# Queries and keys of two chunks by seven products instead of eight, units in pairs of chunks, and the rotation's last two operations on GpSimd

## The chip, the core and the metric

The kernel runs on one core of a Trainium2 chip. The core has five engines, each with its own queue of instructions, done in order: TensorE (PE, matrix products into PSUM; its weight loads are listed as PEld), VectorE (DVE), ScalarE (ACT), GpSimd (POOL) and SyncE (SP, which only issues transfers here). 16 DMA engines move data. SBUF and PSUM are the two memories on the core; PSUM has eight banks of 512 float32 values per partition, and GpSimd works on SBUF only. The metric is the time of one execution in microseconds (us).

## The reference

A transformer block of one attention layer and one small product, in float32, for four sequences (batches) of 1024 tokens with 512 features; 16 heads of 128. Cut to what matters:

```python
xn  = layernorm(x)
q   = apply_rope(rmsnorm(xn @ Wq  + bq,  qn_w), pos)       # 16 heads x 128
lk  = apply_rope(rmsnorm(xn @ Wlk + blk, kn_w), pos)       # local keys
lv  = xn @ Wlv + blv                                       # local values
entries = sum over each 4 tokens of softmax(xn @ Wcmp) * xn
ck, cv  = apply_rope(rmsnorm(entries @ Wk + bk, kn_w), ends), entries @ Wv + bv
sparse  = softmax over the 8 largest of q @ ck.T (causal)  @ cv
local   = softmax over the last 128 keys of q @ lk.T       @ lv
out = x + ((sparse + local) / 2) @ Wo + bo + fp8(xn / 2) @ fp8(input2 / 2) * 4
```

`apply_rope` turns the first 64 of 128 features of a head: with `x1` and `x2` the first and second 32 of them, `x1*cos - x2*sin` and `x1*sin + x2*cos`.

## The kernel before

A *chunk* is 128 tokens, so there are 32 (`NT`), eight per batch (`NCH`). A *unit* is one chunk and two heads, so there are 8 units per chunk (`NU`) and 256 in all (`NN`), numbered chunk by chunk: `place(n)` is `divmod(n, 8)`. The 512 x 512 weights of a unit's queries and keys (two heads of each) lie in `wqk_sb[u]`; they stay in SBUF, as do those of the values (`wlv_sb`) and of the output (`wo_sb`). Biases are folded into the first row of the weights after the first chunk (`fold_first_row`), and the tokens' first row is ones.

The kernel's order is written out by hand (`manual_schedule`): each engine does its instructions in the order in which the program issues them, and waits only on data. A loop over `s` holds the pipeline; step `s` works on several units at once. In the order of issue, step `s` has:

- `scores(s)`, PE (L754, L761, L764): queries times the previous chunk's keys, this chunk's keys, and the compressed keys.
- `keep_context(s-2)`, ACT (L939): copies the context out of PSUM.
- `weigh(s)`: DVE adds masks (L786), finds the eight largest (L807, L812), ACT takes exponentials (L814, L822).
- `queries(s+3)`, PE (L606): four products with the 512 columns of `wqk_sb[u]` into one of two banks `qp`.
- `normalize(s+2)`: DVE multiplies `qp` by `r` and the norm's weight into `th` (L634, four heads), and POOL begins the rotation (L337).
- `settle(s)`, DVE (L830 to L840), and `divide(s)`, ACT (L847, four operations): the probabilities.
- `rotate`'s rest for unit `s+2`, DVE (L339, then L341 and L342).
- `turn(s)`, DVE (L865, two transpositions of `probs` in 32x32 blocks) and a store to DRAM; `turn_keys(s+2)`, DVE (L687, L690) and four stores.
- parts of the preparation of a later chunk (`chunk_prep`: layer norm, transposition, compression), and of `chunk_eight` (the fp8 product), whose quantization is three DVE operations and four of POOL (L292 to L298), one at each call of `steps()`.
- `squares(s+3)` on ACT (L321) and `spread(s+3)` on POOL (L315, L316): sums of squares from `qp`, and from them `r`.
- `to_output(s-2)`, PE (L957); `values_of(s+1)`, PE (L712); `values(s-1)`, PE (L924).
- SP fetches the transposed probabilities (`fetch(s)`, L907) and keys (`fetch_keys(s+2)`, L705) back from DRAM.
- `keep_values(s+1)`, ACT (L724).

In the first eight units the transpositions are made by PE instead (`turn_here`, `turn_keys_here`). A float32 product is listed as two passes on PE. PSUM's eight banks: `qp` two, `sc` two, `pp` two (values and all small products), `out` one, `ctx` one. `scratch` is a tile of 128x512 with two buffers; the preparation's `xb` and the quantization's `qv` and `qm` share it. `ready` and `made` say at which step of which chunk the preparation and the compressed entries of a later one begin.

Of the kernel before, what the change touches and what calls it, by code (L numbers as in the profile page):

```python
# [38 lines left out]
def kernel(  # L39
# [34 lines left out]
    NN = NT * NU  # L74
    assert S // RATIO <= 2 * P and NU == 8 and HID == 512
# [10 lines left out]
    def scratch(name, shape=(P, 512), dtype=F32):  # L86
        return work.tile(list(shape), dtype, tag="scratch", name=name, bufs=2)

    def pp(name):
        return psum.tile([P, 512], F32, tag="pp", name=name, bufs=2)  # L90
# [5 lines left out]
    x_tiles, angles = {}, {}  # L96

    def load_x(t, purpose, extra=False):

        b, c = divmod(t, NCH)  # L100
        if extra:
            xt = scratch(f"x_{purpose}_{t}")
        else:
            xt = work.tile([P, HID], F32, tag="x", name=f"x_{purpose}_{t}")
        nc.sync.dma_start(xt, hidden[b, ts(c, P), :])
        x_tiles[purpose, t] = xt

    def load_angles(t):
        c = t % NCH
        cs = work.tile([P, ROPE], F32, tag="cs", name=f"cs_{t}")  # L110
        nc.sync.dma_start(cs, rope[ts(c, P), :])
        angles[t] = cs
# [10 lines left out]
    wqk_sb = [const.tile([P, KK, 512], F32, name=f"wqk_{u}") for u in range(NU)]  # L123
    wlv_sb = [const.tile([P, KK, 256], F32, name=f"wlv_{u}") for u in range(NU)]
    wo_sb = [const.tile([P, 2, HID], F32, name=f"wo_{u}") for u in range(NU)]

    def load_wqk(u, engine):
        for i, w in enumerate((Wq, Wlk)):
            engine.dma_start(
                wqk_sb[u][:, :, ts(i, 256)], w[:, ts(u, 256)].rearrange("(k p) n -> p k n", p=P)  # L130
            )
# [4 lines left out]
    def load_wo(u, engine):  # L136
        engine.dma_start(wo_sb[u], Wo[ts(u, 256), :].rearrange("(h p) n -> p h n", p=P))
# [13 lines left out]
    for k in range(KK):  # L151
        for i, w in enumerate((Wq, Wlk)):
            nc.sync.dma_start(wqk_sb[0][:, k, ts(i, 256)], w[ts(k, P), 0:256])
# [109 lines left out]
    def fold_first_row(u):  # L263
        w = wqk_sb[u]
        row = first_row.pop(u, None)
        if row is None:
# [3 lines left out]
                row, ident[:, 0:1].to_broadcast([P, P]), w[:, 0, :], start=True, stop=True  # L270
            )
        nc.vector.tensor_tensor(
            w, w, row.unsqueeze(1).to_broadcast([P, KK, 512]), ALU.subtract
        )
        for i, bias in enumerate((bq, blk)):
            nc.sync.dma_start(
                w[0:1, 0, ts(i, 256)], bias[ts(u, 256)].partition_broadcast(1)
            )

# [21 lines left out]
    w2_sb = const.tile([P, KK, HID], BF16, name="w2_sb")  # L301


    w2_raw = [wo_sb[NU // 2 + k][:, 0, :] for k in range(KK)]

    def round_w2():
        for k in range(KK):
            spare = wo_sb[NU // 2 + k][:, 1, :]
# [14 lines left out]
    def rotate(th, cs, nh, a, name, bb=None):  # L323
# [17 lines left out]
        nc.vector.tensor_tensor(x12[:, :, 0, :], a[:, :, 0, :], bb[:, :, 1, :], ALU.subtract)  # L341
        nc.vector.tensor_tensor(x12[:, :, 1, :], a[:, :, 1, :], bb[:, :, 0, :], ALU.add)  # L342


    GC = P // NE
    entries = {}
# [4 lines left out]
    def chunk_prep(t):  # L351
# [46 lines left out]
        log = work.tile([P, 1], F32, tag="log", name=f"log_{t}", bufs=1)  # L398
        row = work.tile([P, 2, BLK], F32, tag="row", name=f"row_{t}", bufs=1)
        red = work.tile([P, BLK // RATIO], F32, tag="red", name=f"red_{t}", bufs=1)  # L400
# [19 lines left out]
        if not t:  # L420
            add_tokens_here(row)
            return
# [21 lines left out]
        else:  # L444
            stores.append((pooled[g][i], few))
        yield "added"
# [31 lines left out]
    def turn_tokens_here(xt):  # L478
# [4 lines left out]
        xnT = work.tile([P, KK, P], F32, tag="xnT", name="xnT_0")  # L483
# [3 lines left out]
    def fetch_tokens(t):  # L487
        xnT = work.tile([P, KK, P], F32, tag="xnT", name=f"xnT_{t}")
# [5 lines left out]
        chunks[t] = xnT, xones[t % 2]  # L494


    xones = [const.tile([P, P], F32, name=f"xone_{i}") for i in range(2)]

    def fetch_with_ones(t):
        turned = tokens.pop(t).rearrange("i (b k) a j -> b i k (a j)", b=NB)  # L500
        for b in range(NB):
            lo = 0 if b else 1
            nc.sync.dma_start(
                xones[t % 2][b * BLK + lo : (b + 1) * BLK], turned[b, lo:, 0, :]
# [92 lines left out]
    def place(n):  # L597

        return divmod(n, NU)

    def queries(n):
        t, u = place(n)
        xnT, xone = chunks[t]
        qp = psum.tile([P, 512], F32, tag="qp", name=f"qp_{n}")
        for k in range(KK):
            nc.tensor.matmul(  # L606
                qp,
# [608 lines left out]
```

## Time and profile before

| what | value |
|---|---|
| median of 3 runs | 2641.59 us (2640.97 to 2642.03) |
| the profiled execution's span, first to last instruction | 2641.7 us |
| PE busy | 2609.3 us |
| DVE busy | 2213.4 us |
| ACT busy | 1390.9 us |
| POOL busy | 786.2 us |
| queries and keys on PE (L606, tokens and ones) | 709.8 + 258.3 us |
| the DMA engines' time taken by the main queue | 58.8% |
| mean granted TensorE clock | 0.999 |

Busy time is the time in which an engine has at least one instruction under way; instructions of one engine overlap a little at their ends. A group's line in the profile names source line, engine, operation, the tile written and those read, the shape and the number of instructions; behind the bar stand busy time, mean duration in ns and idle time before them. A line of the list of waits names the waiting instruction and the one waited for, then total us, number and longest. A line of the timeline names start, duration, engine, line, operation and, in brackets, idle time before it. The span of the profiled execution is as long as the runs' median.

### The profile page before, as it was taken

Reading aid. Unit: us, or ns where it says so; the run is one execution under the profiler, and the core shown is the slowest. Engines: PE = TensorE matmul, PEld = TensorE weight load, DVE = VectorE, ACT = ScalarE, POOL = GpSimd, SP = SyncE. Lnnn points to the kernel's source line nnn. Section 1 sums busy time; section 2 is a strip of 40 time slices with the busy share of each in tenths; the row PEclk is TensorE's granted clock in tenths of the full one; section 3 lists DMA queues with packets and bytes.
Section 4 is the critical chain, followed back from the end, with each engine's and each line's share of the span. In section 5 each row is a group of like instructions: output and inputs, shape, how many; then the busy total and the mean of one; then the engine's idle time right before and its main releaser. Section 6 shows DMA issues by size and latency. Waiting matters only on the chain.

```text
span 2641.7 us, 46868 instructions
## 1 busy us (share of the span) xinstructions
PE 2609.3 (99%) x11879; PEld 1784.3 (68%) x11879; DVE 2213.4 (84%) x8381; ACT 1390.9 (53%) x5560; POOL 786.2 (30%) x1128
## 2 busy tenths in 40 slices
PE   8999999999999999999999999999999999999998
PEld 4666666776666666767766666667666666676776
DVE  6888888889888888888888888888888888877886
ACT  3545545555555555555555555555555555555555
POOL 3522323223332223232233322233323322322222
PEclk9999999999999999999999999999999999999999
DMA  8356556666655555666655555666665555566554
GB/s 255 110 156 162 151 145 175 171 176 158 164 143 154 162 155 156 169 173 170 166 157 144 158 149 158 177 164 164 171 176 147 150 148 153 147 168 171 159 152 110
DMA packets 722252, 422.20 MB, mean 160 GB/s; under 512 B 395823, under 2 KB 671552, under 8 KB 721984
## 3 DMA queue, kind: packets, MB, share of 16 engines
q1 hardware_dynamic: 721952, 419.20, 58.8%
q8 instruction: 97, 1.59, 0.3%
q14 instruction: 171, 1.40, 0.2%
q10 hardware_dynamic: 32, 0.02, 0.0%
HBM read 225.80 MB, written 193.20 MB: 159 GB/s over the span
## 4 chain that ended last, share of the span: by engine, by line
PE 84%; DVE 7%; ACT 3%; DMA 3%; SPq 2%; issue 1%; POOL 0%; ACTq 0%; DVEq 0%
PE qp L606 28%; PE op L957 14%; PE vp L712 14%; PE cp L924 13%; PE sc L764 5%; PE sc L761 4%; PE sc L754 4%; ACT prob L847 1%; ACT prob L814 1%; PE fp L588 1%; DVE sc L786 1%; DVE probB L865 1%; PE ep L536 1%; SPq L695 1%; DVE taken L812 1%
## 5 line engine op out<-in xcount | busy, mean ns | idle before, releaser
L606 PE MATMUL qp<-wqk,xnT 128*128 128x512 f32 x1552 | 709.8, 593 | 3.0 <-DMA wqk<-in_L_attn_Wlk_dram 2.4
L814 ACT ACTIVATE prob<-sc,neg 128x256 f32<-128x256 f32 (+1 forms) x512 | 235.9, 461 | 773.3 <-DVE taken L812 744.0
L606 PEld LDWEIGHTS qp<-wqk,xnT 128*128 128x128 f32 x1552 | 295.0, 190 | 372.5 <-issue 368.8
L847 ACT ACTIVATE prob<-prob,tot 128x256 f32<-128x256 f32 (+7 forms) x1024 | 382.0, 443 | 294.5 <-DVE tot L840 294.5
L712 PEld LDWEIGHTS vp<-wlv,xnT 128*128 128x128 f32 x2048 | 389.0, 190 | 161.3 <-issue 116.2
L957 PE MATMUL op<-wo,cT 128*128 128x512 f32 x1024 | 481.6, 593 | 4.2 <-ACT cT L939 4.2
L712 PE MATMUL vp<-wlv,xnT 128*128 128x256 f32 x2048 | 483.6, 379 | 0.0
L337 POOL TENSOR_TENSOR rb<-th,cs 128x256 f32<-128x256 f32 x256 | 203.8, 796 | 740.0 <-DVE th L634 733.2
L786 DVE CUSTOM_DVE_ANT_0 sc<-sc,mask_b 128x256 f32<-128x256 f32 (+1 forms) x512 | 211.6, 414 | 172.7 <-PE sc L764 162.7
L957 PEld LDWEIGHTS op<-wo,cT 128*128 128x128 f32 x1024 | 193.6, 190 | 229.8 <-issue 186.8
L865 DVE STREAM_TRANSPOSE probB<-prob 128x512 f32<-128x512 f32 (+2 forms) x490 | 305.8, 629 | 11.5
L315 POOL TENSOR_SCALAR r<-ss 128x4 f32<-128x4 f32 x256 | 61.9, 242 | 843.3 <-ACT junk L321 840.6
L924 PE MATMUL cp<-probT,lv 128*128 128x128 f32 x1920 | 299.0, 276 | 6.4 <-DMA probT<-pr 4.9
L321 ACT ACTIVATE junk<-qp 128x128 bf16<-128x128 f32 x1024 | 278.6, 272 | 28.9 <-PE qp L614 4.5
L924 PEld LDWEIGHTS cp<-probT,lv 128*128 128x128 f32 x1920 | 272.8, 191 | 25.4 <-issue 9.3
L634 DVE SCALAR_TENSOR_TENSOR th<-qp,r,norm_w 128x128 f32<-128x128 f32 x1024 | 286.1, 342 | 0.7 <-POOL r L316 0.4
L316 POOL TENSOR_TENSOR r<-r,nhalf 128x4 f32<-128x4 f32 x256 | 265.6, 1037 | 21.4
L830 DVE SCALAR_TENSOR_TENSOR prob<-taken,prob 128x128 f32<-128x128 bf16 (+7 forms) x512 | 186.4, 365 | 98.1 <-ACT prob L822 96.6
L606 PE MATMUL qp<-wqk,xone 128*128 128x512 f32 x496 | 258.3, 602 | 0.9 <-DMA xone<-xb_dram 0.7
L924 PE MATMUL cp<-probT,cv 128*128 128x128 f32 x1536 | 255.1, 275 | 0.0
L764 PE MATMUL sc<-ckT,qT 128*128 128x96 f32 (+7 forms) x1024 | 226.4, 303 | 0.0
L924 PEld LDWEIGHTS cp<-probT,cv 128*128 128x128 f32 x1536 | 212.7, 192 | 0.0
(141 smaller groups left out, 3674.9 us busy)
## 6 DMA issues: line engine op xcount, KB each, us to landing
pr<-probB SPq DMA_DIRECT2D x125, 512.0 KB
probT<-pr SPq DMA_DIRECT2D x500, 128.0 KB
qk<-thb SPq DMA_DIRECT2D x992, 64.0 KB
pr<-probB SPq DMA_DIRECT2D x96, 384.0 KB
probT<-pr SPq DMA_DIRECT2D x384, 96.0 KB
qT<-qk SPq DMA_DIRECT2D x248, 128.0 KB
lkT<-qk SPq DMA_DIRECT2D x248, 128.0 KB
x_norm<-_attn_hidden_states_dram SPq DMA_DIRECT2D x32, 256.0 KB
```

What stands on the lines that cost most here:

```text
L316: nc.gpsimd.tensor_tensor(r, r, nhalf[: ss.shape[0], 0:n], ALU.pow)
L321: nc.scalar.activation(junk[: src.shape[0]], src, AF.Square, accum_out=acc)
L606: nc.tensor.matmul(qp, xnT[:, k, :] if k or not t else xone, wqk_sb[u][:, k, :], start=(k == 0), stop=(t > 0 and k == KK - 1),)
L634: nc.vector.scalar_tensor_tensor(th[:, i, :], qp[:, ts(i, D)], r[:, i : i + 1], norm_w[:, i // 2, :], ALU.mult, ALU.mult,)
L712: nc.tensor.matmul(vp[:, 0:256], xnT[:, k, :], wlv_sb[u][:, k, :], start=(k == 0), stop=(k == KK - 1),)
L764: nc.tensor.matmul(sc[:, spa], q, ckT[:, 0:m], start=True, stop=True)
L786: nc.vector.tensor_tensor_reduce(sc[h][:, loc], sc[h][:, loc], mask_b[:, loc], -1.0, TAKEN, ALU.add, ALU.min, neg[h][0],)
L814: nc.scalar.activation(probs[h][:, loc], sc[h][:, loc], AF.Exp, bias=neg[h][0], scale=-1.0, accum_out=tot[:, h, 0:1],)
L847: nc.scalar.mul(probs[h][:, cols], probs[h][:, cols], tot[:, h, part : part + 1])
L865: nc.vector.transpose(pb[:, :, ds(h * g, g), :], prob[:, parts[0] * P : (parts[-1] + 1) * P].rearrange("p (g b i) -> p b g i", b=NB, i=BLK),)
L924: nc.tensor.matmul(blocks(cp[:, h, :]), v, probT[:, :, h * len(parts) + i - parts[0], :], start=(i == parts[0]), stop=(i == parts[-1]),)
L957: nc.tensor.matmul(op, cT[:, h, :], wo_sb[u][:, h, :], start=(u == 0 and h == 0), stop=(u == NU - 1 and h == 1),)
```

## The change

*Seven products.* For two chunks (256 tokens) and one unit's weights (512 x 512: 256 columns of queries, 256 of keys), the product is a 2x2 scheme of blocks: tokens of chunk a and chunk b, features in two halves, columns in queries and keys. Winograd's form of Strassen's algorithm takes seven block products and fifteen sums. Four sums of weight blocks per unit are made once (`combine_weights`, on POOL in steps 4 to 8), kept in DRAM (`combined`), and loaded for each unit pair into `places`. Four sums of tokens per pair of chunks are made on POOL (`sum_tokens`). The seven sums of results are four on POOL, after four copies by ACT (`first_sums`), and three on DVE straight from PSUM (`second_sums`). The first two chunks are computed as before.

*Order of units.* From the 17th unit on, units of two chunks alternate: chunk 2p unit u, chunk 2p+1 unit u. In an even step `first_products` (four products of 256 columns, two halves each) takes the place of `queries`, in an odd step `second_products` (three); they fill four quarters of two banks, `qk_banks`. `squares` and `normalize` read `th` in SBUF then, and `normalize` writes it in place.

*Rotation.* The last two operations of `rotate` (L341, L342) go to GpSimd for the units; the compressed keys' stay on DVE.

*Buffers.* `out` has two banks, `pp` one, and values and context share one (`vc`). `wo` is not kept whole but loaded per unit, then per unit pair, into two tiles. `scratch` has four buffers, `th` three tiles, tokens four. Preparation, entries and loads get new steps (`prep_at`, `made`, `tokens_at` and others), one chunk's preparation spread over six steps.

The diff, cut to its core:

```diff
+    def row_of_weights(u, k):
+        return wqk_sb[u][:, k // 2, :, k % 2, :]
...
+    def combine_weights(u):
+        (b11, b12), (b21, b22) = (
+            [flat(wqk_sb[u][:, j, i]) for i in range(2)] for j in range(2)
+        )
+        one, two = (v.rearrange("p h d -> p (h d)") for v in th_tiles[1:])
+        sub = nc.gpsimd.tensor_tensor
+        sub(one, b12, b11, ALU.subtract)
+        nc.sync.dma_start(combined[u][0], one)
+        sub(two, b22, one, ALU.subtract)
+        nc.sync.dma_start(combined[u][1], two)
+        sub(one, b21, two, ALU.subtract)
+        nc.sync.dma_start(combined[u][3], one)
+        sub(two, b22, b12, ALU.subtract)
+        nc.sync.dma_start(combined[u][2], two)
+    places = [flat(wqk_sb[u][:, 0, 1]) for u in range(NU)]
...
+    def load_combined(u, which):
+        for i in which:
+            nc.sync.dma_start(places[i], combined[u][i])
+    def sum_tokens(p, which):
...
+        op = nc.gpsimd.tensor_tensor
+        if which == 0:
+            op(s3, a11, a21, ALU.subtract)
+            op(s1, a21, a22, ALU.add)
+            op(s2, s1, a11, ALU.subtract)
+        else:
+            op(s4, a12, s2, ALU.subtract)
...
-        nc.vector.tensor_tensor(x12[:, :, 0, :], a[:, :, 0, :], bb[:, :, 1, :], ALU.subtract)
-        nc.vector.tensor_tensor(x12[:, :, 1, :], a[:, :, 1, :], bb[:, :, 0, :], ALU.add)
+        adder = nc.gpsimd if nh > 1 else nc.vector
+        adder.tensor_tensor(x12[:, :, 0, :], a[:, :, 0, :], bb[:, :, 1, :], ALU.subtract)
+        adder.tensor_tensor(x12[:, :, 1, :], a[:, :, 1, :], bb[:, :, 0, :], ALU.add)
...
-        return divmod(n, NU)
+        if n < FIRST:
+            return divmod(n, NU)
+        p, r = divmod(n, FIRST)
+        return 2 * p + r % 2, r // 2
...
+    def first_products(p, u):
+        xa, one = chunks[2 * p]
+        s1, s2, s3, _ = token_sums
+        t1, t2, t3, _ = (v.rearrange("p (k n) -> p k n", k=2) for v in places[:4])
+        lo, hi = qk_banks
+        product(lo[:, 0:256], (one, xa[:, 1, :]), wqk_sb[u][:, 0, 0])
+        product(hi[:, 256:512], both(s1), t1)
+        product(lo[:, 256:512], both(s2), t2)
+        product(hi[:, 0:256], both(s3), t3)
+    def second_products(p, u):
+        xa, xb = chunks[2 * p][0], chunks[2 * p + 1][0]
+        lo, hi = qk_banks
+        product(lo[:, 0:256], both(xa[:, 2:4, :]), wqk_sb[u][:, 1, 0])
+        product(hi[:, 0:256], both(xb[:, 2:4, :]), places[3].rearrange("p (k n) -> p k n", k=2))
+        product(hi[:, 256:512], both(token_sums[3]), wqk_sb[u][:, 1, 1])
...
+    def first_sums(n):
+        for i in (n, n + 1):
+            units[i] = {"th": pools["th"].take(i)}
+        c11, c12, c21, c22 = quarters(n)
+        lo, hi = qk_banks
+        nc.scalar.copy(c11, lo[:, 0:256])
+        nc.scalar.copy(c22, lo[:, 256:512])
+        nc.scalar.copy(c21, hi[:, 0:256])
+        nc.scalar.copy(c12, hi[:, 256:512])
+        nc.gpsimd.tensor_tensor(sums, c11, c22, ALU.add)
+        nc.gpsimd.tensor_tensor(c21, c21, sums, ALU.add)
+        nc.gpsimd.tensor_tensor(c22, c21, c12, ALU.add)
+        nc.gpsimd.tensor_tensor(c12, c12, sums, ALU.add)
+    def second_sums(n):
+        c11, c12, c21, _ = quarters(n)
+        lo, hi = qk_banks
+        nc.vector.tensor_tensor(c11, c11, lo[:, 0:256], ALU.add)
+        nc.vector.tensor_tensor(c21, c21, hi[:, 0:256], ALU.add)
+        nc.vector.tensor_tensor(c12, c12, hi[:, 256:512], ALU.add)
...
+    prep_at = {1: -1, 2: 6, 3: 8, 4: 13, 5: 16, 6: 19, 7: 22}
...
+        if s + 3 < FIRST:
+            for_unit(s + 3, (queries,))
+        if strassen and s != FIRST - 4:
+            (second_products if odd else first_products)(*pair_of)
...
         if s + 2 >= NU:
             for_unit(s + 2, (turn_keys,))
+        if strassen:
+            (second_sums if odd else first_sums)(2 * pair)
         steps()
-        host = t if u < 4 else t + 1
...
+        prepare(s, 0)
         for_unit(s + 3, (squares, (0, 1, 2, 3)), (spread,))
         for_unit(s - 2, (to_output,))
         steps()
+        prepare(s, 1)
...
+        if 0 <= s <= FIRST:
+            load_wo(s, nc.sync)
+        elif s > FIRST and odd:
+            load_wo(s + 1, nc.sync)
...
+        for v in {4: (0, 1), 5: (2, 3), 6: (4, 5), 7: (6,), 8: (7,)}.get(s, ()):
+            combine_weights(v)
+        if s == FIRST - 5:
+            load_combined(0, range(4))
+            spare_banks[:] = [pp_bank]
+        if strassen:
+            if odd:
+                load_combined((pair_of[1] + 1) % NU, (3,))
+            else:
+                load_combined((pair_of[1] + 1) % NU, (0, 1, 2))
```

## The prediction

> **What bounds the kernel now.** I read the page first: how long each engine is busy. Then the list of waits: who waits for whom. Then the timeline of single steps, to see how far the second-busiest engine is from the first.
>
> ```profile
> span 2641.7 us, 46868 instructions
> PE 2609.3 (99%) x11879; PEld 1784.3 (68%) x11879; DVE 2213.4 (84%) x8381; ACT 1390.9 (53%) x5560; POOL 786.2 (30%) x1128
> ```
>
> PE sets the pace. DVE is not 16% behind it, though, because part of DVE's idle time is spent on answers from ACT. What DVE waits for PE is this:
>
> ```profile
> DVE sc L786 <- PE sc L764: 162.7, 166, 2.1
> ...
> DVE qm_x L288 <- DMA pooled<-xb: 8.8, 3, 3.3
> DVE xb L378 <- DMA pooled<-xb: 7.8, 3, 2.6
> ...
> PE cp L924 <- DMA probT<-pr: 4.9, 9, 0.9
> ```
>
> So a PE of no length would leave 2641.7 - 162.7 = 2479.0 us: DVE's own line, 6% under the span. The reader should also see two short waits for a buffer (`scratch`), and that transfers arrive just in time (4.9 us in nine waits).
>
> PE's prices, from one step of the third chunk (columns: start, duration, engine, line):
>
> ```profile
> 1503.90 1.05 PE L606 MATMUL qp<-wqk,xone 128*128 128x512 f32 x2
> ...
> 1504.79 2.74 PE L606 MATMUL qp<-wqk,xnT 128*128 128x512 f32 x6
> ...
> 1507.36 1.03 PE L588 MATMUL fp<-w_sb,x 128*128 128x512 bf16 x4
> ...
> 1509.94 1.89 PE L712 MATMUL vp<-wlv,xnT 128*128 128x256 f32 x8
> ...
> 1511.67 0.61 PE L924 MATMUL cp<-probT,lv 128*128 128x128 f32 x4
> ```
>
> Starts count, since ends overlap. Four products of 512 columns are 8 passes and take 1507.36 - 1503.90 = 3.46 us, 0.4325 each; eight passes of 256 columns take 1511.67 - 1509.94 = 1.73 us, 0.216 each: exactly half, and longer than the 0.19 us of a weight load.
>
> DVE's step, between the reciprocal and the next step (fourth chunk):
>
> ```profile
> 1626.41 0.18 DVE L840 RECIPROCAL tot<-tot 128x4 f32<-128x4 f32 x1
> 1626.59 0.42 DVE L339 TENSOR_TENSOR thb<-th,cs 128x256 f32<-128x256 f32 x1
> 1626.68 1.49 ACT L847 ACTIVATE prob<-prob,tot 128x256 f32<-128x256 f32 x4 [0.87 <-DVE tot L840]
> ...
> 1627.12 0.29 DVE L341 TENSOR_TENSOR th<-thb,rb 128x128 f32<-128x128 f32 x1
> 1627.32 0.28 DVE L342 TENSOR_TENSOR th<-thb,rb 128x128 f32<-128x128 f32 x1
> 1627.53 1.26 DVE L865 STREAM_TRANSPOSE probB<-prob 128x384 f32<-128x384 f32 x2
> ...
> 1628.71 0.40 DVE L687 STREAM_TRANSPOSE thb<-th 128x256 f32<-128x256 f32 x1
> ...
> 1629.03 0.40 DVE L690 STREAM_TRANSPOSE thb<-th 128x256 f32<-128x256 f32 x1
> ...
> 1631.09 0.43 DVE L786 CUSTOM_DVE_ANT_0 sc<-sc,mask_b 128x256 f32<-128x256 f32 x1 [1.65 <-PE sc L764]
> ```
>
> The reader should see that ACT's four divisions end at 1628.17, and that the second half of L865 (about 0.6 of its 1.26 us) needs the last of them. The two rotation operations at 1627.12 and 1627.32 run while ACT divides.
>
> **The change, part by part.** One profiled execution lasts 2641.7 us; the runs' median is 2641.59, so nothing has to be added. 120 of the 128 unit pairs use the new products.
>
> *PE.* A pair took 16 x 0.4325 = 6.92 us and will take 28 x 0.216 = 6.05 (7 products, 2 halves, 2 passes): -0.87, times 120 = -104. PE's line becomes 2537.
>
> *DVE, three sums a pair.* The nearest row is `kv<-ep,bkv_sb` (L547), 128x256 from PSUM and SBUF, 0.386 us alone. In a row, L634 (0.343) comes every 0.26, so 0.31 apart: 0.31 + 0.31 + 0.386, less the overlap with what goes before, 0.95. +114 (bounds 84, for 0.7, and 139, for three times 0.386).
>
> *Rotation's end on GpSimd.* It takes 0.41 us from DVE per unit (1627.12 to 1627.53), 98 us over 240 units if all of it were on the path. By the rows above ACT covers it, and the transposition still waits until 1628.17: I take 0, bounds 0 and -98. On POOL the two cost some 0.46 each (L337: 0.322 for 64 elements, 0.732 for 256), done before L687 starts, so no new wait there. Normalizing from SBUF instead of PSUM is shorter at most; the second L830 waits 0.41 for ACT anyway.
>
> *ACT.* Four copies a pair at L724's 0.366: +176 on 1390.9, inside its idle time. But on ACT's queue the squares stand behind them, and in odd steps behind DVE's sums.
>
> *POOL.* Four sums of 0.73 and four rotation operations a pair: 4.8 x 120 = +570; busy share about 55%. What counts is what it holds up:
>
> ```profile
> 1567.16 1.28 POOL L294 TENSOR_TENSOR qv_x<-qv_x,qm_x 128x512 f32<-128x512 f32 x1
> ...
> 1567.36 1.11 DVE L839 TENSOR_SCALAR tot<-tot 128x4 f32<-128x4 f32 x1
> ```
>
> L839 takes 0.17 us and is held until POOL's operation ends. All L839s take 92.6 us instead of 256 x 0.170 = 43.5. After the change the quantization's POOL operations stand behind the rotation, which comes after L839: -45 (bounds 0 and -49). In exchange they stand in front of `r`. Third chunk, even step, from the start of L786: reciprocal ends at 5.0, divisions at 6.6, two copies at 7.4, POOL's four sums at 10.3, `r` (0.2 + 1.03) at 11.6; the next normalization is due at about 9.2 + 2.5 = 11.7. With L294 (1.27) and L296 (0.62) in between it is 1.8 late, of which ACT's 0.41 covers part: 1.4 per chunk. The sum of `x` and the bias adds some 0.6, chunk preparation on DVE and POOL's sums holding each other another 1.0. 3.0 x 30 chunks = +90. Bounds: 0, since L634 today is 0.343 beside any POOL operation, and +180, twice as much. I take the middle because `normalize` will read only SBUF, as L839 does.
>
> [...]
>
> *Start.* Combining weights is 32 POOL operations of 1.27 us; two of four also wait some 0.7 for a store of the buffer that they overwrite: 6.45 a unit, 52 in steps 4 to 8. In that stretch (77.0 to 140.9) POOL is busy 27.7 of 63.9 us; 36 are free, the rotation needs 5, and the units' `r` and rotation queue behind. At least 52 - 31 = 21; I take +25 (0 to 40). The four `scratch` buffers end the waits for `pooled`: -17 (0 to -17), hidden by nothing, since DVE waits hardly for PE there.
>
> *Transfers.* 1.5 MB a pair (four combined weights, one `wo`): 189 MB. The fullest slice moves 255 GB/s, so 740 us of the queue's time at that pace, on top of 58.8% of the span: over 80%. They are issued on SP behind `fetch_keys`, when SP waits for the next L865. 0 taken; bounds 0 and +60.
>
> *PSUM waits.* `first_products` waits for the first of the three sums only. PE's odd step is short (6.0 us plus scores and values, 8.8 in the third chunk), and DVE reaches that sum at 7.8 + 0.4 = 8.2 in the third chunk: no wait in itself.
>
> Sum on DVE's line: 2479.0 + 114 + 0 - 45 + 90 + 25 - 17 = 2646, plus a twentieth of today's waits for PE (8): **2654 us**.
>
> **Rivals.**
> - *The gain stays* (the other side). DVE's step gets shorter by the rotation: place L865, price 98 us. It decides if L865 after the change starts and ends earlier by over 0.2 us after the reciprocal. Then DVE's line is near 2556 and PE's is 2537 + 25 - 17 = 2545; with some of the lateness left, 2580. For: 0.41 us fewer instructions. Against: 1628.17.
> - *Transfers become late.* The store of `probB` queues behind combined weights; today a fetch is issued by 1507.4 and used about 1511.7. If half of 240 steps slip by 0.5 us: +60, 2714. For: the share over 80%. Against: only 4.9 us of such waits today.
> - *Half as wide is not half as long*, so the change saves PE nothing: 2700. Against: L712.
>
> **How the numbers follow.** DVE's line decides: 0.46 (own range 2635 to 2680); the gain stays: 0.34; transfers: 0.15; the last: 0.05. The range, 2585 to 2715, takes in half the rotation's bound below (-49 and the chunk term 20 smaller) and the transfer term above. About 0.2%, 5.3 us, is what a measurement can tell: faster 0.34 + 0.06 of the first case's lower end = 0.40; within 0.2% 0.09; slower 0.51.
>
> **What would show it.** Right: PE's busy share falls to some 96%, L606 is replaced by 256-column groups of 0.216 us spacing; DVE's share rises past 86% and its waits for PE's scores nearly vanish; L839's mean drops towards 0.17; L865 still ends 2.2 us after the reciprocal; PE waits for DVE's sums or POOL's results; steps 4 to 8 are longer. Wrong: PE still at 99% with a span below 2590 (then DVE had more room than I count), or new PE waits for `probT` or `qT`.

## The result and the profile after

The changed kernel takes 3030.1 us (median of 4 runs, 3028.9 to 3037.2), the kernel before, measured beside it, 2641.3 us: a ratio of 1.148 (95% interval 1.146 to 1.150). Slower was forecast, at 2654 us with a range up to 2715. The size is off by 376 us. The direction held, but slower had been given a chance of 0.51 and faster one of 0.40, so that says little.

The head of the page of the changed kernel:

```profile
span 3028.7 us, 52949 instructions
...
PE 2717.5 (90%) x13266; PEld 2124.7 (70%) x13301; DVE 2261.3 (75%) x8229; ACT 1567.8 (52%) x6032; POOL 1421.8 (47%) x2198
```

PE's share fell further than the 96% forecast, and not because DVE took over: DVE's share fell too, from 84% to 75%. PE is even busy 108 us longer than before, in part at a lower clock (below), although its queries and keys now need 28 passes of 256 columns a pair instead of 16 of 512. No engine is busy throughout; all of them wait. The list of waits (waiting instruction, the one waited for, total us, number, longest):

```profile
DVE thb L868 <- POOL th L434: 146.3, 20, 9.6
...
DVE sc L970 <- PE sc L946: 125.7, 81, 13.4
...
PE qk L743 <- DVE th L791: 123.3, 67, 6.1
...
DVE probB L1049 <- ACT prob L1031: 116.6, 231, 0.7
ACT th L779 <- DVE thb L868: 115.6, 108, 1.2
DVE th L814 <- POOL r L407: 108.9, 92, 5.6
...
DVE x L464 <- POOL off L459: 64.6, 16, 4.8
...
PE qk L743 <- DMA wqk<-combined: 35.4, 22, 3.9
...
PE vc L1115 <- DMA probT<-pr: 22.0, 25, 2.1
```

Before, DVE waited for PE's scores (162.7 us), for ACT's exponentials (96.6 us) and for little else. Now DVE waits for POOL in three places (L868, L814, L464: 319.8 us), PE for DVE (123.3 us), DVE for PE: a ring. A quiet step of a batch's third chunk, with the beginning of the next step, still looks much as forecast (start, duration, engine, line):

```profile
1108.84 2.75 PE L743 MATMUL qk<-wqk,wqk 128*128 128x256 f32 x12
...
1113.82 0.18 DVE L1024 RECIPROCAL tot<-tot 128x4 f32<-128x4 f32 x1
1114.00 0.43 DVE L430 TENSOR_TENSOR thb<-th,cs 128x256 f32<-128x256 f32 x1
1114.09 1.44 ACT L1031 ACTIVATE prob<-prob,tot 128x256 f32<-128x256 f32 x4 [0.91 <-DVE tot L1024]
1114.57 0.45 POOL L433 TENSOR_TENSOR th<-thb,rb 128x128 f32<-128x128 f32 x1 [1.11 <-DVE thb L430]
...
1114.90 1.25 DVE L1049 STREAM_TRANSPOSE probB<-prob 128x384 f32<-128x384 f32 x2 [0.48 <-ACT prob L1031]
...
1116.07 0.40 DVE L868 STREAM_TRANSPOSE thb<-th 128x256 f32<-128x256 f32 x1
...
1121.90 1.14 DVE L814 SCALAR_TENSOR_TENSOR th<-th,r,norm_w 128x128 f32<-128x128 f32 x4 [1.13 <-POOL r L407]
```

Twelve products of 256 columns take 2.75 us, 0.216 apart. The reciprocal ends at 1114.00, ACT's divisions end at 1115.53, the transposition L1049 cannot end before that: the rotation, taken from DVE, had been in ACT's shadow. And in the last line `r` is 1.1 us late. Elsewhere the same ring breaks wide open. Step 11 of each 16, same view:

```profile
1151.05 0.72 POOL L356 TENSOR_TENSOR wqk<-tokens,tokens 128x256 f32<-128x256 f32 x1 [8.79 <-DMA tokens<-xb_dram]
...
1154.91 0.45 DVE L868 STREAM_TRANSPOSE thb<-th 128x256 f32<-128x256 f32 x1 [6.96 <-POOL th L434]
...
1156.04 1.78 PE L743 MATMUL qk<-wqk,tokens 128*128 128x256 f32 x4 [4.01 <-DVE th L791]
...
1157.61 3.84 PE L743 MATMUL qk<-wqk,wqk 128*128 128x256 f32 x12
```

POOL waits 8.8 us for a transfer of tokens, DVE's transposition 7 us for POOL, PE 4 us for DVE. The twelve products after that take 3.84 us instead of 2.75: the clock has dropped. The granted clock is 1.00 from 1146.2 to 1156.0 us, 0.50 from 1156.4 to 1159.7, and 1.00 again from 1160 on. The view of the cores gives its mean:

```profile
core 0: 3028.7 us, clock 0.968
```

It was 0.999 before. A loss of 3.2% of 3029 us is 97 us of full clock, or 194 us at half. PE is busy in only 149 of these 194 us, so the lower clock makes PE's own work longer by some 75 us at most, and how much of that lies on the path no run shows. The Trainium skill (TensorE: Matmul & The Clock Gate, Part 1, "What's actually happening") says that the clock is halved after an idle window of some 3.4 us. The 3.84 us behind a gap of 4.0 us agree; no run here measures the window.

The steps' lengths, counted between first starts of the mask operation (L786, now L970), locate the loss: the first 16 steps take 245.5 us instead of 176.2 (+69); the later groups of 16 some 171 to 195 instead of 148 to 172, some 22 more each, 14 times.

### The profile page after: what moved, and what is told of

It is laid out like the page before. It is cut to its first block, busy times and chain, and to the rows that moved or that the text cites. A ratio compares the mean times of both kernels' runs of the same rounds, so it can differ in the third digit from the quotient of the medians.

```text
span 3028.7 us, 52949 instructions
## 1 busy us (share of the span) xinstructions
PE 2717.5 (90%) x13266; PEld 2124.7 (70%) x13301; DVE 2261.3 (75%) x8229; ACT 1567.8 (52%) x6032; POOL 1421.8 (47%) x2198
## 3 DMA queue, kind: packets, MB, share of 16 engines
q1 hardware_dynamic: 828176, 621.15, 71.9%
## 4 chain that ended last, share of the span: by engine, by line
DVE 28%; PE 28%; ACT 15%; POOL 10%; issue 8%; DMA 8%; SPq 4%; ACTq 0%; POOLq 0%; DVEq 0%
PE qk L743 8%; ACT prob L1031 7%; PE vc L1115 5%; PE out L1146 4%; PE vc L894 4%; DVE prob L1014 3%; DVE sc L970 3%; ACT prob L998 3%; DVE th L814 3%; DMA pr<-probB 2%; DVE taken L996 2%; DVE thb L868 2%; DVE top L991 2%; POOL r L407 2%; DMA wqk<-combined 2%
## 5 line engine op out<-in xcount | busy, mean ns | idle before, releaser
L743 PE MATMUL qk<-wqk,tokens 128*128 128x256 f32 x1440 | 385.3, 402 | 184.5 <-DVE th L791 123.3
L1146 PE MATMUL out<-wo,cT 128*128 128x512 f32 x1024 | 501.3, 613 | 53.9 <-ACT cT L1131 50.6
L894 PEld LDWEIGHTS vc<-wlv,tokens 128*128 128x128 f32 x2048 | 393.3, 192 | 171.7 <-issue 125.7
L894 PE MATMUL vc<-wlv,tokens 128*128 128x256 f32 x2048 | 488.5, 382 | 4.7 <-ACT lv L906 4.7
L743 PE MATMUL qk<-wqk,wqk 128*128 128x256 f32 x1860 | 466.1, 397 | 3.9 <-DMA wqk<-combined 3.9
L412 ACT ACTIVATE junk<-th 128x128 bf16<-128x128 f32 x960 | 299.4, 312 | 298.0 <-DVE th L791 275.0
L743 PEld LDWEIGHTS qk<-wqk,tokens 128*128 128x128 f32 x1440 | 262.5, 195 | 246.7 <-DVE th L791 141.1
L743 PEld LDWEIGHTS qk<-wqk,wqk 128*128 128x128 f32 x1860 | 374.7, 202 | 62.6 <-issue 4.6
L1049 DVE STREAM_TRANSPOSE probB<-prob 128x512 f32<-128x512 f32 (+2 forms) x490 | 310.0, 633 | 135.7 <-ACT prob L1031 116.6
L814 DVE SCALAR_TENSOR_TENSOR th<-th,r,norm_w 128x128 f32<-128x128 f32 x960 | 307.3, 381 | 103.3 <-POOL r L407 103.1
L1115 PE MATMUL vc<-probT,lv 128*128 128x128 f32 x1920 | 314.3, 283 | 23.8 <-DMA probT<-pr 22.0
L970 DVE CUSTOM_DVE_ANT_0 sc<-sc,mask_b 128x256 f32<-128x256 f32 (+1 forms) x510 | 209.6, 411 | 134.6 <-PE sc L946 125.7
L1115 PE MATMUL vc<-probT,cv 128*128 128x128 f32 (+3 forms) x1536 | 292.6, 291 | 0.0
```

What stands on the lines that cost most here:

```text
L412: nc.scalar.activation(junk[: src.shape[0]], src, AF.Square, accum_out=acc)
L743: nc.tensor.matmul(to, a[k], b[:, k, :], start=k == 0, stop=k == 1)
L814: nc.vector.scalar_tensor_tensor(th[:, i, :], qp[:, i, :], r[:, i : i + 1], norm_w[:, i // 2, :], ALU.mult, ALU.mult,)
L894: nc.tensor.matmul(vp, xnT[:, k, :], wlv_sb[u][:, k, :], start=(k == 0), stop=(k == KK - 1),)
L970: nc.vector.tensor_tensor_reduce(sc[h][:, loc], sc[h][:, loc], mask_b[:, loc], -1.0, TAKEN, ALU.add, ALU.min, neg[h][0],)
L1049: nc.vector.transpose(pb[:, :, ds(h * g, g), :], prob[:, parts[0] * P : (parts[-1] + 1) * P].rearrange("p (g b i) -> p b g i", b=NB, i=BLK),)
```

## The experiments

Each is one run of a kernel beside one of the kernel before, which stayed between 2638.0 and 2640.9 us. The changed kernel's four times spread over 8 us, so differences of that size tell nothing. Where no other base is named, the edit is made on the changed kernel (3030).

### The line of the diff that was not costed: values over fewer rows

The change also shortens the contraction in `values` to the compressed entries that exist. Alone, on the kernel before:

```diff
-                    v = cv[i - 2]
+                    v, rows = cv[i - 2], min(P, m - P * (i - 2))
...
-                    v,
-                    probT[:, :, h * len(parts) + i - parts[0], :],
+                    v[0:rows],
+                    probT[0:rows, :, h * len(parts) + i - parts[0], :],
```

> The kernel before with one line of the change alone: values contracts the compressed entries over the rows that exist (32, 64, 96 or 128) instead of always over 128. In the changed kernel's trace passes over 32 or 64 rows come 0.21 us apart and passes over 96 or 128 rows 0.11, and value products take 477 us by the distance of their starts where the kernel before has 389. Theory A (this line alone costs PE some 88 us, and PE is busy 99%): 2715 to 2745. Rival (the longer passes belong to the bank that the changed kernel shares between two products, not to the rows): within 10 us of 2640.

2729.5 us: +88.6. PE's busy time rises by 92 us. The groups of these products, shapes apart (rows * columns of the weights; behind the bar busy time, mean ns):

```profile
L924 PE MATMUL cp<-probT,cv 128*128 128x128 f32 x768 | 138.0, 275 | 0.0
L924 PE MATMUL cp<-probT,cv 64*128 64x128 f32 x256 | 62.1, 322 | 0.0
L924 PE MATMUL cp<-probT,cv 32*128 32x128 f32 x256 | 61.9, 321 | 0.0
L924 PE MATMUL cp<-probT,cv 96*128 96x128 f32 x256 | 49.5, 274 | 0.0
```

Fewer rows are slower, not faster: 0.32 us for 32 or 64 rows against 0.27 for 96 or 128. Passes overlap, so the distance of their starts says more. In the changed kernel, two passes of 32 rows and two of 96 rows, each between passes of 128 (start, duration):

```profile
117.25 0.48 PE L1115 MATMUL vc<-probT,cv 32*128 32x128 f32 x2
117.66 0.49 PE L1115 MATMUL vc<-probT,lv 128*128 128x128 f32 x2
118.08 0.48 PE L1115 MATMUL vc<-probT,cv 32*128 32x128 f32 x2
...
1149.59 0.39 PE L1115 MATMUL vc<-probT,cv 96*128 96x128 f32 x2
1149.81 0.61 PE L1115 MATMUL vc<-probT,lv 128*128 128x128 f32 x4
```

Two passes of 32 rows take 0.41 us from start to start, two of 96 rows 0.22. In h4, too, a pass of 32 or 64 rows starts 0.20 to 0.21 us after the pass before it, and so does the pass behind it; all others come 0.11 us apart. Added up, these distances are some 85 us more in h4 than before, which is nearly all of the loss. In the changed kernel, taken back:

```diff
-                    v, rows = cv[i - 2], min(P, m - P * (i - 2))
+                    v, rows = cv[i - 2], P
```

> The changed kernel with that line taken back: values over 128 rows always. Theory A (PE's passes lie on the ring of waits, PE being busy 90%): 30 to 97 us faster, 2935 to 3000, more of it in chunks with 32 or 64 rows. Rival (the ring runs through POOL and DVE, PE's passes are in shadow): within 15 us of 3030.

3027.2 us: no difference, though PE is busy 55 us less (2662.7). The rival holds: where PE waits, the time it saves becomes waiting (PE's wait for L791 grows from 123.3 to 154.8 us). (The line belongs to the pairs: the two chunks of a pair take turns on the same tiles of probabilities, and the one with fewer entries finds what the other left behind. Kernels with pairs and 128 rows take that into the sum, so that part of their output differs from the reference's.)

### Strassen taken out, the pairs left

```diff
-        strassen = pair >= NU and pair < NN // 2
+        strassen = False
...
-        if s + 3 < FIRST:
-            for_unit(s + 3, (queries,))
+        for_unit(s + 3, (queries,))
```

with the combining, the loads of combined weights and the sums of tokens left out too.

> Undoes Strassen alone: every unit's queries and keys come from four full products of 512 columns again, with no combined weights, no sums of tokens and no sums of products; the pairs of chunks, the loads and the rotation on POOL stay as in the changed kernel. Theory A (the 389 us come from what Strassen's sums add to POOL, ACT and DVE and from the waits around them): 2600 to 2690, near the kernel before. Rival (working in pairs of chunks, with its bursts of transfers and of chunk preparation, disturbs the staging by itself): above 2800.

2751.1 us, between the two, with PE busy 98%: PE is the bound, and longer by 97 us. With the contraction over 128 rows:

> As g1_pairs_alone (pairs of chunks and rotation on POOL, without Strassen), with values over 128 rows always. Theory A (g1's 111 us above the kernel before are this line): 2645 to 2680. Rival (working in pairs costs by itself): above 2710.

2671.2 us: -80. So pairs, loads and rotation together cost some 30 us, the short contraction 80, and the remaining 279 us belong to Strassen. This split depends on the order: with 128 rows on both sides Strassen costs 356 us (h1 against h2), because the short contraction counts only where PE is the bound. What in it?

### Single waits taken away

*Tokens fetched four steps earlier:*

```diff
-        tokens_at.update({FIRST * p - 8: 2 * p, FIRST * p - 7: 2 * p + 1})
+        ahead = 12 if p > 1 else 8
+        tokens_at.update({FIRST * p - ahead: 2 * p, FIRST * p - ahead + 1: 2 * p + 1})
```

> Only change: from the second pair of chunks on, the turned tokens are fetched four steps earlier. Theory A (the sums of tokens stand at the head of POOL's queue in step 11 of 16 and wait there for these transfers, DVE's transposition waits for POOL, PE for DVE, and the clock drops behind the gap): step 11, now 18.8 us, falls to about 10, so 14 times 9 us less, 2905 (2890 to 2930), and the wait of POOL L356 for the transfer (58.9 us) vanishes. Theory B (POOL and DVE are simply crowded, the work comes to the same wherever the wait is): the time moves by less than 30 us.

2966.5 us: -64, half of what was expected. Step 11 falls from 18.8 to 12.6 us (here and below the mean over the groups of 16 from the third on), not to 10, and POOL's wait for the transfer (L356) from 58.9 to 10.3 us. The waits of this run:

```profile
DVE th L814 <- POOL r L407: 121.0, 88, 5.5
...
DVE thb L868 <- POOL th L434: 41.0, 7, 9.6
```

L868 lost 105 us of its waits; L814's grew by 12.

*The rotation back on DVE:*

```diff
-        adder = nc.gpsimd if nh > 1 else nc.vector
+        adder = nc.vector
```

> Only change: the last two operations of the rotation are on DVE again. Theory A (they were in the shadow of ACT's divisions on DVE, and on POOL they stand in front of the sums and of r): faster by 20 to 80 us, 2950 to 3010, with the waits of DVE L868 for POOL L434 (146.3 us) gone and less idle time in front of L814. Rival (DVE sets the pace, 0.41 us a unit come back): slower by 50 to 98 us.

3059.0 us: slower by 29, against the theory and short of the rival's range. DVE gets 125 us busier (2386.0), and the wait only changes its name; it stays with POOL's first rotation operation:

```profile
DVE th L433 <- POOL rb L428: 162.8, 22, 9.3
```

So the move to POOL was worth 29 us net, of the 98 us that it took off DVE.

*Small operations of the preparation on DVE:*

```diff
-            nc.gpsimd.tensor_scalar(off[:, 0:1], st[:, 6:7], -1.0, None, ALU.mult)
+            nc.vector.tensor_scalar(off[:, 0:1], st[:, 6:7], -1.0, None, ALU.mult)
```

and L459 likewise.

> Only change: the two small operations of chunk preparation (L455, L459) run on DVE instead of POOL. Theory A (they stand behind the four sums of the pair and DVE's L464 waits for them, 64.6 us, and ACT's L456): faster by 40 to 70 us, 2960 to 2990. Rival (DVE then waits behind the sums for r instead, the wait only moves): within 20 us of 3029.

3013.1 us: -17, the rival's range. Step 6 falls from 14.7 to 12.5 us, but step 15 grows from 10.6 to 11.5. Early tokens, this edit and the 128 rows together:

> The changed kernel with three parts mended: tokens fetched four steps earlier (63 us alone), the two small operations of chunk preparation on DVE (16 us alone), values over 128 rows. If the three add up: 2860 to 2920. Rival (each sits in the same ring and hides the others): above 2930.

2956.6 us: -74; the parts add up to -64 - 17 - 3 = -84, so they nearly add. The time lies in the rival's range, but not for the rival's reason: the forecast had counted on the rows.

*The start.* One unit's weights combined per step:

```diff
-        for v in {4: (0, 1), 5: (2, 3), 6: (4, 5), 7: (6,), 8: (7,)}.get(s, ()):
+        for v in range(s - 4, s - 3) if 4 <= s < 12 else ():
```

> Only change: the weights are combined one unit a step in steps 4 to 11 instead of two a step in 4 to 6. Theory A (two units a step are 16 us of POOL in a step of 9 and r waits behind them): faster by 20 to 45 us, 2985 to 3010, and the tenth step starts near 165 us instead of 191. Rival (POOL's work and waits for stores are the same wherever they are): within 10 us of 3029.

3032.3 us, the first 16 steps 246.8 us: no difference. The timeline of steps 6 to 7 in the changed kernel shows why:

```profile
105.94 0.45 POOL L434 TENSOR_TENSOR th<-thb,rb 128x128 f32<-128x128 f32 x1
...
107.80 1.12 DVE L814 SCALAR_TENSOR_TENSOR th<-qk,r,norm_w 128x128 f32<-128x128 f32 x4 [5.62 <-POOL r L407]
...
111.21 1.27 POOL L333 TENSOR_TENSOR th<-wqk,th 128x512 f32<-128x512 f32 x1
111.22 1.28 DVE L1023 TENSOR_SCALAR tot<-tot 128x4 f32<-128x4 f32 x1
...
112.63 3.44 DVE L309 TENSOR_TENSOR wqk<-wqk,first_row 128x1024 f32<-128x1024 f32 x2
...
115.06 2.16 POOL L337 TENSOR_TENSOR th<-wqk 128x512 f32<-128x512 f32 x1
...
122.82 1.26 POOL L337 TENSOR_TENSOR th<-wqk 128x512 f32<-128x512 f32 x1 [0.71 <-DMA combined<-th]
...
125.73 0.45 DVE L868 STREAM_TRANSPOSE thb<-th 128x256 f32<-128x256 f32 x1 [8.23 <-POOL th L434]
```

`r` and the rotation stand in POOL's queue among the combining operations, so neither placing hides the 1.3 us apiece. DVE's L1023, 0.17 us alone, takes 1.28 beside one of them (L333). It goes the other way too: POOL's L337 takes 2.16 us where it begins beside DVE's L309, and 1.26 later on.

### `r` ahead of the sums

*On the base of the early tokens, squares and `r` ahead of `first_sums`:*

```diff
-        if strassen:
-            (second_sums if odd else first_sums)(2 * pair)
...
+        if strassen and odd:
+            second_sums(2 * pair)
+        if pair >= NU:
+            for_unit(s + 3, (squares, (0, 1, 2, 3)), (spread,))
+        if strassen and not odd:
+            first_sums(2 * pair)
...
```

> Tokens fetched early as in e1_tokens_early, and in addition the squares and r of the unit come before the first sums of the next pair on ACT and on POOL. Theory A (in even steps r stands behind four sums of 0.73 us, and behind quantization; DVE's normalization waits for it, 121 us): 2850 to 2910, with the wait of L814 for POOL below 50 us. Rival (the wait moves on: the copies of the first sums now come two us later, and the second products or DVE's sums wait for them): within 25 us of 2966.

2987.1 us: 21 slower than without. The wait at L814 falls from 121.0 to 7.1 us. PE's waits for the copies (L780) rise from 13.2 to 50.9 us, as the rival has it, and DVE's at L464 from 64.7:

```profile
DVE x L464 <- POOL off L459: 131.5, 30, 6.6
```

Two variants of it. A fourth `th` tile (`sums` takes the tile of the rotation's `rb`):

```diff
-    th_tiles = [const.tile([P, 4, D], F32, name=f"th_{i}") for i in range(3)]
+    th_tiles = [const.tile([P, 4, D], F32, name=f"th_{i}") for i in range(4)]
```

> As f1_r_first, with a fourth tile for queries and keys (the sum's own tile is shared with the rotation's to make room), so that ACT's copies need not wait for DVE's transposition. Theory A (copies that wait make the second products and the squares late): 20 to 60 us faster than f1_r_first. Rival (ACT has room, 52% busy, and the copies' wait is hidden): within 15 us of f1_r_first.

2990.2 us: no difference. ACT's wait at L779, 115.6 us in the changed kernel, is already 1.6 us in f1, so what it costs there is not shown. And the combining on DVE:

```diff
-        sub = nc.gpsimd.tensor_tensor
+        sub = nc.vector.tensor_tensor
```

> As f1_r_first, with the weights combined on DVE (32 operations at about 0.6 us instead of 1.3 on POOL). Theory A (at the start POOL's queue holds r behind the combining): 25 to 50 us faster than f1_r_first, and the first 16 steps, 245 us, fall to about 205. Rival (the start waits for transfers and stores, not for POOL): within 12 us of f1_r_first.

3010.9 us: 24 slower than f1; the first 16 steps take 268.0 us, 249.7 in f1. DVE's operations now wait for the stores of their two tiles (45.4 us), and nothing else of DVE runs meanwhile.

f1 with L455 and L459 on DVE as well, edited as above:

> As f1_r_first (tokens early, squares and r ahead of the first sums), with the two small operations of chunk preparation on DVE. In f1 what r gained was lost at L464, which waited 131.5 us for those operations behind the sums (step 6: 16.6 us against 15.0). Theory A (that was the whole of f1's loss): 2850 to 2895. Rival (the squares ahead of the copies make the second products late instead): 2930 or more.

2951.0 us, 36 better than f1, the rival's range, and within 6 us of h3 (2956.6), which has `r` behind the sums and 128 rows. Instead of that order, early tokens and L455 and L459 on DVE with POOL's sums moved to the beginning of the odd step:

```diff
+    def middle_sums(n):
+        c11, c12, c21, c22 = quarters(n)
         nc.gpsimd.tensor_tensor(sums, c11, c22, ALU.add)
...
+        if strassen and odd:
+            middle_sums(2 * pair)
         for_unit(s + 2, (normalize,))
```

> Tokens early, the two small operations on DVE, and POOL's four sums of a pair moved from the end of the even step to the beginning of the odd step, when DVE weighs and POOL is idle; the copies stay first on ACT, and r no longer stands behind the sums. Theory A (r behind POOL's queue is the largest wait left: 137 us at L814 in h3): 2790 to 2860. Rival (DVE and POOL hold each other wherever the sums are, and DVE's own operations get longer): within 30 us of 2950.

2977.3 us, the rival's range. And with the sums left out, where they were:

```diff
-        nc.gpsimd.tensor_tensor(sums, c11, c22, ALU.add)
-        nc.gpsimd.tensor_tensor(c21, c21, sums, ALU.add)
-        nc.gpsimd.tensor_tensor(c22, c21, c12, ALU.add)
-        nc.gpsimd.tensor_tensor(c12, c12, sums, ALU.add)
```

> Tokens early, the two small operations on DVE, and POOL's four sums of a pair left out, so that queries and keys are not those of the reference; copies, products and DVE's three sums stay. It prices all that the four sums cost: their place in the queue and their port. Theory A: 2750 to 2830, near k2 or a little below. Rival (POOL's sums do not matter, DVE's sums and ACT's copies do): 2920 or more.

2880.4 us, between theory and rival. The normalization's groups (count, busy time, mean ns of one, idle time before them) tell these orders apart; first e1 and f1, which differ by the order alone, then k2 and k4:

```profile
L814 DVE SCALAR_TENSOR_TENSOR th<-th,r,norm_w 128x128 f32<-128x128 f32 x960 | 326.7, 401 | 115.6 <-POOL r L407 115.3
```

```profile
L814 DVE SCALAR_TENSOR_TENSOR th<-th,r,norm_w 128x128 f32<-128x128 f32 x960 | 406.2, 483 | 1.5 <-POOL r L407 1.5
```

```profile
L817 DVE SCALAR_TENSOR_TENSOR th<-th,r,norm_w 128x128 f32<-128x128 f32 x960 | 469.7, 548 | 22.6 <-POOL r L407 21.5
```

```profile
L810 DVE SCALAR_TENSOR_TENSOR th<-th,r,norm_w 128x128 f32<-128x128 f32 x960 | 309.8, 383 | 16.0 <-POOL r L407 14.9
```

From e1 to f1 the wait for `r` falls by 114 us, and the operation itself gets longer by 80: it now runs beside POOL's sums. In k2 it meets them oftener: 548 ns. Without the sums it takes 383 ns and waits 16 us. The traces show the holding one by one: a normalization that meets no operation of POOL takes 343 to 345 ns in the changed kernel, h3, k1, k2 and k4, and in k2 one beside a sum takes 743 to 837 ns in the mean, depending on which of the four. In the kernel before, where it reads PSUM, it stays at 342 or 343 beside POOL's operations.

So the sums cost some 75 us (k4 against h3, which has the same two mends, but 128 rows). Three orders were tried, with `r` behind the sums (h3, 2956.6), with `r` ahead (k1, 2951.0) and with the sums in the odd step (k2, 2977.3), and none bought it back: late and held came to nearly the same. The Trainium skill (SBUF — State Buffer, "Who interferes with whom") says that a DVE instruction with two SBUF inputs contends with a GpSimd instruction that reads SBUF, and that the order of issue decides which of them blocks. The normalization has two such inputs only in the changed kernel, and the numbers above agree.

### What remains without any sum

On k4, DVE's sums left out as well:

```diff
-            (second_sums if odd else first_sums)(2 * pair)
+            if not odd:
+                first_sums(2 * pair)
```

> As k4_no_pool_sums, with DVE's three sums of a pair left out as well: the products go to their banks and are copied, and nothing adds them up, so queries and keys are not those of the reference. Theory A (DVE's sums, 0.95 us a pair, lie on the ring, as the prediction's +114 has it, and the first products wait for them): 2740 to 2800. Rival (copies, transfers and the start carry the rest): 2850 or more.

2874.0 us, 6 less than k4: the rival. Once POOL's sums are gone, DVE's three cost nothing that can be told; with POOL's sums in place it was not tried. With 128 rows:

> As k5_no_sums, with values over 128 rows always (the rows beyond the entries then meet probabilities that the other chunk of the pair left, so that part of the output changes too). If PE sets the pace once the sums are gone, the 88 us of the short contraction come back in full and PE's saving shows: 2640 to 2710, with PE busy 96% or more. Rival (something else holds: DVE, transfers): within 30 us of k5.

2858.1 us, the rival's range. Neither the sums of products nor the short rows are left, and the kernel is still 187 us above the same kernel without Strassen (h2). ACT's copies, the sums of tokens, the combining and the loads of combined weights remain. PE is busy as long as in h2 (2611.8 and 2612.4 us): the saving does not show, in part because 109 us of PE's busy time lie at half the clock (26 in h2). Of the 187 us, 53 lie in the first 16 steps (236.0 us against 183.2 in h2). For the rest, PE's waits in k6:

```profile
PE qk L743 <- DMA wqk<-combined: 107.2, 84, 4.6
...
PE vc L1111 <- DMA probT<-pr: 46.0, 70, 2.4
```

and the transfer queue's own, before, in h2 and in k6:

```profile
SPq L907 <- DMA pr<-probB: 24.2, 37, 1.4
```

```profile
SPq L1098 <- DMA pr<-probB: 78.4, 95, 2.7
```

```profile
SPq L1094 <- DMA pr<-probB: 290.4, 203, 4.0
```

PE waits 153 us for these transfers (25.7 in h2, for `probT`). All of PE's waits together are 188 us longer than in h2 (238 against 50), so transfers are 128 of that. The fetch of the transposed probabilities waits 290 us on SP for its own store, 78 in h2 and 24 before: stores and fetches, combined weights and `wo` share one queue, whose transfers fill 76.2% of the engines' time (66.5% in h2, 58.8% before). This is read from the waits, not tested by itself: no run took the loads away, and none took away ACT's copies or the sums of tokens. One run bears on it: on the base of k2, the pairs' combined weights on ACT's queue:

```diff
-    def load_combined(u, which):
+    def load_combined(u, which, queue=nc.sync):
...
-            nc.sync.dma_start(places[i], combined[u][i])
+            queue.dma_start(places[i], combined[u][i])
...
-                load_combined((pair_of[1] + 1) % NU, (3,))
+                load_combined((pair_of[1] + 1) % NU, (3,), nc.scalar)
...
```

> As k2_sums_later, with the combined weights loaded from ACT's queue instead of SP's. Theory A (on SP they stand behind transfers that wait, so PE waits 44 us for them in h3, with a clock drop behind each of the longer waits): 10 to 40 us faster than k2. Rival (ACT's queue has waits of its own, or the transfers' time is the engines' and not the queue's): within 10 us of k2.

3195.1 us, 218 slower than k2, outside both expectations:

```profile
PE vc L1118 <- DMA probT<-pr: 283.7, 112, 8.7
```

PE's wait for the probabilities goes from 31 to 284 us, and by the profile SP's fetch of them waits 248 us for loads of combined weights, which now stand in the other queue. That speaks for the transfers' time rather than the order on SP as the limit, but it is one run, and what a second queue itself changes is not separated from it.

The ladder, in us: 2641 before; 2671 pairs (h2); 2751 with the short contraction (g1); 3030 with Strassen. Back down: 2957 with tokens, preparation and rows mended (h3); 2880 without POOL's sums (k4, short rows); 2874 without DVE's (k5); 2858 with 128 rows (k6). No run was faster than the kernel before.

## Why the prediction was right and wrong

Two steps of the prediction failed. The first is its frame: the sum adds everything on DVE's line, as if DVE set the end and nothing else could become late. DVE was to rise past 86% and fell to 75%; the engines wait for each other in a ring. The second is the size of two terms in it, *Lateness* (+90, where the runs took away 156 us) and *Transfers* (0, where 134 us remain in k6 behind the sums, beside PE's waits for transfers). The signs that came out are the 0.216 us and the transposition ending 2.2 us after the reciprocal; DVE's waits for PE's scores did not vanish (125.7 us).

*PE, -104.* The price was right (0.216 apart). What failed is the list of edits: the shorter contraction is in the diff and stands in no term. It costs 88 us by itself, so PE's own line was 2625, not 2537, and little was left to gain. In the changed kernel it happened to cost nothing (h1), since PE waits.

*Three sums on DVE, +114.* The durations fit (L791 to L793 0.31 apart, the last 0.41). That they lie on the path is not borne out: k5 took them out, after POOL's sums, and gained 6.

*Rotation, 0.* Mostly right: L1049 waits for ACT 231 times, 116.6 us. The move's worth here is -29 (e2), inside the bounds.

*L839, -45.* Right: its successor L1023 fell from 362 to 221 ns in the mean, 36 us.

*Lateness, +90.* The right kind, the wrong size and partly the wrong place. Found were 64 for tokens, 17 for the preparation, 75 for POOL's sums: 156, with more that only moved between L814, L464 and L868. The token sums at the head of POOL's queue in step 11, and the transfers they wait for, were not in the walk at all. And lateness was added up on DVE's line as if it stayed there; PE waits for the first of DVE's sums (123.3 us at L791), so it passes on, and behind the longer gaps the clock drops with it, at most some 75 us of PE's work and in no term.

*Start, +25 - 17.* Mis-sized: +69 is what the first 16 steps grew by, 60 of it against the pairs alone (185.1). Of 52 us of combining, 31 were taken to lie beside POOL's idle time. None seems to have been hidden, since `r` and the rotation queue behind it: spreading it changed nothing (e3), and without the sums the first 16 steps are still 53 us above h2 (k6). No run left the combining out by itself.

*Transfers, 0, at most 60.* The largest single error, as far as the runs go. Of k6's 187 us above h2, 134 lie after the start, and PE waits 128 us more for transfers than in h2. That these waits make the 134 us is read from the profile and was not tested, so their cause stays open to that extent. The rival *transfers become late* (2714) has this mechanism at a smaller price: half the steps, 0.5 us each. The share of the engines' time that it was argued from did not rise past 80%, but to 71.9% (76.2% in k6). In the changed kernel itself PE waits only 35.4 and 22.0 us for these transfers; that the rest is hidden behind the sums is the likely reading.

*First products wait for nothing.* Wrong: PE waits 123.3 us for L791, in 67 of 120 pairs and up to 6.1 us. In itself the step leaves room, as walked; every late DVE step uses it up.

*The other rivals.* *The gain stays* did not come true. That half as wide is not half as long is refuted by L743's 0.216 us.

## What to carry to other kernels

Cost every line of a diff, also one that looks like a saving: a shorter contraction was 88 us slower by itself. Before moving work to an engine with idle time, walk its queue through a whole period, the odd steps with their transfers and preparations first; what stands behind the moved work there is late everywhere. An engine that is 30% busy is no free place for operations that hold a busy engine's: here being late (2957 us) and being held (2951 us) cost the same.

## What the runs showed of the hardware

*Rows.* In a chain of products over 128 rows, a pass over 32 or 64 rows starts 0.20 to 0.21 us after the pass before it, and so does the pass after it; beside passes over 96 or 128 rows it is 0.11 (h4). The mean durations are 321 and 322 ns against 274 and 275. The Trainium skill (TensorE: Matmul & The Clock Gate, "Why this matters for your kernels") says that a single product over 32 rows takes as long as one over 128. Here, in a chain, it does not; the measurement decides. The switch between row counts is not all of it: between two passes over the same 32 rows it is 0.21 us as well.

*Holding works both ways.* A DVE operation of 128x4 elements took 1.28 us beside a GpSimd operation of 128x512 (0.17 alone), and a GpSimd operation of 128x512 took 2.16 us where it began beside a DVE operation with two SBUF inputs (1.26 otherwise). The normalization took 548 ns in the mean instead of 383.

*A second queue.* Moving loads of 256 KB from SP's queue to ACT's made another transfer late, by 252 us in PE's waits (k3 against k2).
